# Two fused graph layers: the first layer's turns by transposing DMA instead of TensorE

## The chip, the core and the metric

The kernel runs on one core of one Trainium2 chip. The engines in the text are PE (TensorE, matrix products and transposes into PSUM), DVE (VectorE), ACT (ScalarE), POOL (GpSimd) and SP (SyncE, which here issues every DMA, in order). The metric is device time in microseconds of one execution, as the median of several runs. Trace times come from one profiled execution of the kernel.

## The reference

128 graphs of 64 nodes with 768 features pass through two layers, each of the form `layernorm(x + layer(x))`. Cut to what is computed:

```python
# layer 0: graph attention, 12 heads of 64
h = einsum('bnd,ade->bane', x, W); th = tanh(h)
attn = th @ w_src + swap(th @ w_dst)             # [b, a, n, m]
attn = where(attn >= 0, attn, 0.2 * attn)
attn = softmax(where(~adj, -999.0, attn), axis=-1)
f = elu(merge_heads(attn @ h) + b)
gate = sigmoid(x @ H_w.T + H_b)
x = layernorm(x + gate * f + (1 - gate) * x)
# layer 1: masked self-attention, 6 heads of 128
q, k, v = x @ Wq + bq, x @ Wk + bk, x @ Wv + bv
probs = softmax(q @ k.T / sqrt(128) + where(adj, 0, -9e15))
x = layernorm(x + (probs @ v) @ Wf + bf)
```

All is float32. Two graphs make a tile of 128 rows; there are 64 tiles.

## The kernel before

**Products.** The dense products are done by a Strassen-like scheme with seven products instead of eight on blocks of 128 tokens x 384 features and 384 x 384 weights. Two tiles, A and B, make a pair (32 pairs); a matrix times a pair is seven products (P1, P6, P5, P2, P7, P3, P4), each of three matmuls in the code and six PE instructions in the trace, summed in three PSUM banks. The weights' sums are prepared once: w0 and h_w by DVE, wv by POOL, and wq, wk, wf by POOL in `to_there`, which writes them to DRAM for phase B. The tokens' sums come from POOL, with DVE's help.

**Phase A** is layer 0 and the `v` of layer 1. For each pair p it emits `hidden(p)` (h and tanh, seven products, trace name h), `gate(p)` (g), and `value(p - 1)` (v). **Phase B** is the rest of layer 1, with the products q, k and o.

**The order by ticks.** The program is one hand-made order. `Beat.product` emits one product and then calls `tick`, which emits the reads of the product before and lets every open line (a generator) go on if its count is over. So a tick is the time of one product. `Beat.until(...)` ticks without emitting a product until something has been emitted. Each engine executes its own instructions in that order.

**A tile's attention** is the line `attend`, started when the last product that it needs has been read. Its steps and their ticks stand in `TICKS` (for the first pair, `FIRST_TICKS`): `targets` and `sources` on POOL; `spread`, which writes the sums to DRAM and reads them back spread over partitions (`bc`); `masked`, `greatest`, `shifts`, `lesser`, `shifted` on DVE; two exps on ACT; `greater` on DVE, whose result `d` is the softmax's numerator. Then `turn_weights` turns `d` by six PE transposes into the PSUM tile `turn` (L643), `weights` copies it to SBUF with ACT (L651), and `first_means`, `last_means` use it as the stationary operand of 24 small matmuls (`f_ps`, L665). After division, ELU, gate, sum and normalization (`normal`, ACT, L717), `turn_rows` stores the row block and turns it again by six PE transposes, and `rows` copies it into `x1b` (L727), from which `value` takes its blocks. When both tiles of a pair are turned, their sums are formed and all blocks are stored to `ops_there` for q and k.

PSUM has eight banks: four for the dense sums, two for `turn`, two for `f_ps`. The small masks and shifts of the softmax lie in unused columns of `turn`. One buffer of eight blocks (`x1b`) holds a pair's turned rows. The region `zone` in SBUF is shared by x's blocks, `to_there` and phase B's operands.

At the end of phase A the order is h31, g31, v30, then q and k of the first quad of tiles (with wq, wk and their blocks loaded from DRAM), then v31.

Of the kernel before, what the change touches and what calls it, by code (L numbers as in the profile page):

```python
# [29 lines left out]
F32 = mybir.dt.float32  # L30
U8 = mybir.dt.uint8
AF = mybir.ActivationFunctionType
ALU = mybir.AluOpType
# [39 lines left out]

TICKS = (0, 2, 2, 2, 4, 6, 7, 7, 8, 8, 10, 10, 10, 11, 12, 14, 14, 15, 15, 16, 16, 17, 18, 19, 19, 19, 20, 21, 23)

FIRST_TICKS = (0, 1, 1, 1, 3, 4, 4, 5, 5, 5, 5, 5, 5, 7, 7, 8, 8, 8, 8, 9, 9, 10, 11, 13, 13, 14, 16, 16, 16)
AFTER_A, AFTER_B = 0, 2
# [48 lines left out]
def two_layers(  # L126
# [29 lines left out]
    dram = ctx.enter_context(tc.tile_pool(name="dram", bufs=1, space=DRAM))  # L156
    dense = ctx.enter_context(tc.tile_pool(name="dense", bufs=4, space=PSUM))
    tiny = ctx.enter_context(tc.tile_pool(name="tiny", bufs=3))
# [37 lines left out]
    def to_there(w, name):  # L196
        blocks = w.rearrange("(k c p) (m n) -> k m c p n", k=2, p=P, m=2)
        for c in range(KH):
            t = in_zone(6 * D, 7, HALF)
            for at, k, m in ((W11, 0, 0), (T3, 0, 1), (W22, 1, 1), (W21, 1, 0)):  # L200
                nc.sync.dma_start(t[:, at], blocks[k, m, c])
            yield 6
            for half in (t[:, :, 0 : HALF // 2], t[:, :, HALF // 2 : HALF]):
                yield from sums_of_weights(nc.gpsimd, half)
                yield 1
            yield 3
            nc.sync.dma_start(w_there[name][:, :, c, :], t)
            yield 8

# [16 lines left out]
    def per_head(ap, k):  # L226

        return ap.unsqueeze(2).to_broadcast([P, ap.shape[1], k])

    def row(w, name, pool):  # L230
        t = pool.tile([P, w.shape[0]], F32, name=name)
        nc.sync.dma_start(t, w.partition_broadcast(P))
        return t
# [10 lines left out]
    def by_token(name, blocks, w, reads):  # L244

        sums = [sb(dense, [P, BANK], "dense", f"{name}{i}") for i in range(3)]
        begun = set()
        for what, to, xb, wb in TURNS:
            ps = sums[to][:, 0:HALF]

            def emit():
                for c in range(KH):
                    nc.tensor.matmul(  # L253
                        ps,
                        lhsT=blocks[xb][:, c, :],
                        rhs=w[:, wb, c, :],
                        start=(c == 0 and to not in begun),
                        stop=(c == KH - 1),
                        skip_group_check=True,
                    )  # L260

            read = reads[what]
            beat.product(emit, lambda read=read, ps=ps: read(ps))
            begun.add(to)
# [30 lines left out]

    ready = {}
    quads = {q: {"q": q} for q in range(n_quads)}
# [17 lines left out]
    def by_feature(name, blocks, w, f, b_sb, r, part, then=None):  # L315

        sums = [sb(dense, [P, BANK], "dense", f"{name}{i}") for i in range(3)]
        begun = set()
# [47 lines left out]
    def phase_a(pa, ps_a, dst_pool):  # L366
# [199 lines left out]
        def attend(S):  # L566
# [72 lines left out]

            def turned_from(rows):  # L640
                held["turn"] = True
                for c in range(KC):
                    nc.tensor.transpose(turn[:, c * P : (c + 1) * P], rows[:, c * P : (c + 1) * P], ident)  # L643

            def turn_weights():
                turned_from(d)


            def weights():
                S["sT"] = tmp(f"sT_{t}")  # L650
                nc.scalar.copy(S["sT"], turn[:, 0:D])  # L651
                held["turn"] = False

            def means(first, last):
                def work():
                    if first == 0:
                        held["f"] = True
                        S["f_ps"] = sb(ps_a, [P, 2 * BANK], "f", f"f_ps_{t}", 1)
                    for hd in range(first, last):
# [3 lines left out]
                        for b in range(2):  # L663
                            rows = slice(r * N, (r + 1) * N)
                            nc.tensor.matmul(  # L665
                                S["f_ps"][b * N : (b + 1) * N, at : at + E0 + 1],
                                lhsT=S["sT"][rows, hd // 2 * P + b * N : hd // 2 * P + (b + 1) * N],
                                rhs=(h[rows, hd, 0 : E0 + 1] if r == b else hx[rows, hd // 2, 0 : E0 + 1]),
# [8 lines left out]
            def divided():  # L677
                f_ps = S["f_ps"].rearrange("p (r n) -> p r n", r=2)[:, :, 0 : 6 * EP]
                f_ps = f_ps.rearrange("p r (c e) -> p r c e", c=6)
# [35 lines left out]
            def normal():  # L715
                rs = S["rs"]
                nc.scalar.activation(S["f"], S["f"], AF.Identity, bias=rs[:, 1:2], scale=rs[:, 0:1])  # L717

            def turn_rows():
                nc.sync.dma_start(x1_there[t], S["f"])  # L720
                turned_from(S["f"])

            def rows():
                if p not in x1_all:
                    x1_all[p] = sb(pa, [P, 8, KH, P], "x1b", f"x1b_{p}", 1)
                to = x1_all[p][:, 2 * side : 2 * side + 2].rearrange("p k c t -> p (k c t)")
                nc.scalar.copy(to, turn[:, 0:D])  # L727
                held["turn"] = False

            steps = [  # L730
                targets, target_sums, spread, sources, source_sums, masked, greatest, shifts, biased,
                beside, lesser, shifted, lesser_exp, shifted_exp, greater, turn_weights, weights,
                first_means, last_means, divided, below, unit, gated, summed, measured, power_of,
                normal, turn_rows, rows,
            ]

            place = {turn_weights: "turn", turn_rows: "turn", first_means: "f"}
            now = 0
            for step, at in zip(steps, TICKS if p else FIRST_TICKS):
                if at > now:  # L740
                    yield at - now
                    now = at
                while step in place and held[place[step]]:
                    yield 1
                step()
            turned[p] = turned.get(p, 0) + 1
            if turned[p] == 2:
                yield 1
                xo = x1_all[p]
                x1_blocks[p] = [xo[:, i] for i in range(8)]  # L750
                sums = xo[:, S1 : S4 + 1]
                yield from sums_of_tokens(nc.gpsimd, sums, *x1_blocks[p][0:4], first=nc.vector)
                yield 1
                there = ops_there[p // 2][:, p % 2]
                nc.sync.dma_start(there[:, 0 : 2 * KH], xo[:, 0:2].rearrange("p k c t -> p (k c) t"))
                nc.sync.dma_start(there[:, 2 * KH : 7 * KH], xo[:, 3:8].rearrange("p k c t -> p (k c) t"))

        x1_all, x1_blocks, turned = {}, {}, {}


        turn = ps_a.tile([P, 2 * BANK], F32, name="turn")
        held = {"turn": False, "f": False}

        def masks(p, A, B):
# [3 lines left out]
            for i, S in enumerate((A, B)):  # L768
                at = D + i * P
                parts = [turn[:, at : at + N]]  # L770
                parts += [turn[:, at + N + k * H0 : at + N + (k + 1) * H0] for k in range(3)]
                S["aside"], S["a8"] = parts, a8[:, i]

        def first_blocks():
            for _, _, xb, _ in TURNS:
                yield 2 if xb == S4 else 1
                blocks[xb] = load_block(0, xb)

        for p in range(n_pairs):
# [14 lines left out]
            elif p:  # L794
                beat.start(matrix("wk"), 6)
                beat.start(first_blocks())
            if p:
                beat.until(lambda: p - 1 in x1_blocks)
                value(p - 1)

        beat.until(lambda: "wq_sb" in ready and len(blocks) == 7)
        queries(0, 0, blocks, part)
        beat.until(lambda: "wk_sb" in ready)
        keys(0, 0, blocks, part)
        beat.until(lambda: n_pairs - 1 in x1_blocks)
        value(n_pairs - 1)
        beat.drain()

    blocks = {}
    with (  # L810
        tc.tile_pool(name="pa", bufs=1) as pa,
        tc.tile_pool(name="ps_a", bufs=1, space=PSUM) as ps_a,
        tc.tile_pool(name="dst_there", bufs=1, space=DRAM) as dst_pool,
        tc.manual_schedule(),
    ):
        phase_a(pa, ps_a, dst_pool)


    def phase_b(pb, ps_b):
# [3 lines left out]
        def last_bias():  # L823

            for m, parts in enumerate((((0, W11), (1, W21)), ((0, W11), (0, T1), (1, W22)))):
                ps = sb(dense, [P, BANK], "dense", f"bias_ps_{m}")[:, 0:HALF]
                steps = [(k * KH + c, wb, c) for k, wb in parts for c in range(KH)]
# [209 lines left out]
    with (  # L1037
        tc.tile_pool(name="pb", bufs=1) as pb,
        tc.tile_pool(name="ps_b", bufs=1, space=PSUM) as ps_b,
        tc.manual_schedule(),  # L1040
    ):
        phase_b(pb, ps_b)

# [46 lines left out]
```

## Time and profile before

| | |
|---|---|
| median of 2 runs | 3020.57 us (3020.05 to 3021.09) |
| profiled execution | 3020.48 us, span 3018.7 us, granted clock 0.995 |
| PE busy | 2973.2 us (98%) |
| DVE / ACT / POOL busy | 1956.1 / 778.2 / 1065.3 us |
| DMA, share of 16 engines | 36.3% on the hardware queue |
| phase A ends (last product v31) | about 1518 us |
| transposes on PE | 768 instructions, 0.27 us each, in 128 groups of six |

A group in the profile is all instructions of one line, engine and operation; `out<-in` are the program's tile names. "Idle before" is the time the engine stood before them and what released it. The chain is followed back from the last instruction to what released each step. A busy share is an average over stages: phase A and phase B have different second engines (DVE is busy 861 of 1000 us from 400 to 1400 us, and 230 of 500 from 2200 to 2700).

### The profile page before, as it was taken

What the parts mean: (1) busy time and instruction counts of PE and PEld (TensorE: products, weight loads), DVE (VectorE), ACT (ScalarE), POOL (GpSimd) and SP (SyncE); (2) the same over time, 40 slices, a digit from 0 to 9 for tenths busy, and PEclk for the clock granted to TensorE, in tenths of its full rate; (3) what the DMA queues carried; (4) which work ended last, traced back from release to release, by engine and by line L of the source; (5) the groups of instructions that cost most, each with busy time, mean ns of one, the idle gap of its engine ahead of it and who ended that gap; (6) DMA issues with size and microseconds to landing.
All of it is one profiled execution on the core that took longest, in us unless ns stands there. A gap on an engine that the chain in (4) does not pass through costs nothing.

```text
span 3018.7 us, 43164 instructions
## 1 busy us (share of the span) xinstructions
PE 2973.2 (98%) x16542; PEld 2071.7 (69%) x16542; DVE 1956.1 (65%) x3664; ACT 778.2 (26%) x1201; POOL 1065.3 (35%) x1006
## 2 busy tenths in 40 slices
PE   7999999999999999999899999999999999999998
PEld 4666666556666666666677787877878778787785
DVE  6888888888888888888634444444444454444444
ACT  2334334333333333333211111111111111111111
POOL 4556665564554554554202211112111121111212
PEclk9999999999999999999999999999999999999999
DMA  5444645534434434434741332222322223232131
GB/s 169 153 156 146 196 141 172 182 125 128 142 111 130 142 110 131 142 107 135 241 140 53 90 101 79 79 66 77 101 79 85 74 63 100 79 97 78 58 100 42
DMA packets 283311, 347.01 MB, mean 115 GB/s; under 512 B 90593, under 2 KB 226657, under 8 KB 283105
## 3 DMA queue, kind: packets, MB, share of 16 engines
q1 hardware_dynamic: 283104, 344.25, 36.3%
q8 instruction: 130, 2.13, 0.3%
q14 instruction: 77, 0.62, 0.1%
HBM read 199.07 MB, written 132.32 MB: 110 GB/s over the span
## 4 chain that ended last, share of the span: by engine, by line
PE 94%; DVE 2%; DMA 2%; issue 1%; ACT 0%; POOL 0%; SPq 0%; DVEq 0%; POOLq 0%; ACTq 0%
PE k L349 15%; PE o L253 14%; PE q L349 14%; PE h L253 14%; PE g L253 13%; PE v L253 13%; PE c_ps L907 3%; PE turn L643 3%; PE f_ps L665 2%; PE s_ps L867 2%; PE sT_ps L896 1%; DMA there<-dst 0%; DMA bc<-there 0%; DMA zone<-in_xT 0%; PE bias_ps L829 0%
## 5 line engine op out<-in xcount | busy, mean ns | idle before, releaser
L253 PE MATMUL h<-w_sb,zone 128*128 128x384 f32 x1344 | 464.2, 494 | 9.3 <-DMA w_sb<-in_w 6.7
L349 PE MATMUL q<-zone,wq_sb 128*128 128x256 f32 x2016 | 462.5, 382 | 1.6 <-DVE q_u L325 1.5
L253 PE MATMUL g<-h_w_sb,zone 128*128 128x384 f32 x1344 | 446.3, 488 | 7.5 <-DVE g L516 7.5
L349 PE MATMUL k<-zone,wk_sb 128*128 128x256 f32 x2016 | 453.6, 381 | 0.0
L253 PE MATMUL v<-wv_sb,x1b 128*128 128x384 f32 x1344 | 443.9, 489 | 8.3 <-DVE v L545 4.2
L349 PEld LDWEIGHTS q<-zone,wq_sb 128*128 128x128 f32 x2016 | 377.2, 190 | 60.2 <-DVE q_u L325 2.4
L349 PEld LDWEIGHTS k<-zone,wk_sb 128*128 128x128 f32 x2016 | 378.8, 190 | 55.5 <-DVE zone L335 4.7
L253 PEld LDWEIGHTS v<-wv_sb,x1b 128*128 128x128 f32 x1344 | 255.8, 191 | 190.9 <-issue 16.9
L253 PEld LDWEIGHTS g<-h_w_sb,zone 128*128 128x128 f32 x1344 | 251.2, 191 | 170.2 <-DVE g L516 8.1
L253 PEld LDWEIGHTS h<-w_sb,zone 128*128 128x128 f32 x1344 | 246.9, 191 | 162.2 <-issue 9.3
L947 POOL TENSOR_TENSOR y<-y,bf_sb 128x768 f32<-128x768 f32 x64 | 114.9, 1816 | 498.3 <-DMA y<-x_there 414.9
L960 POOL TENSOR_TENSOR o<-o,y 128x384 f32<-128x384 f32 x96 | 107.4, 1119 | 499.3 <-issue 250.6
L253 PE MATMUL o<-wf_sb,sc 128*128 128x384 f32 x768 | 268.0, 493 | 2.8 <-DVE sc L239 2.8
L277 POOL TENSOR_TENSOR rs<-rs,power 128x1 f32<-128x1 f32 x128 | 71.4, 558 | 538.6 <-DVE rs L275 538.6
L253 PEld LDWEIGHTS o<-wf_sb,sc 128*128 128x128 f32 x768 | 144.1, 191 | 100.0 <-DVE sc L239 3.8
L253 PE MATMUL o<-wf_sb,cT 128*128 128x384 f32 x576 | 201.8, 487 | 0.5 <-ACT cT L921 0.5
L493 POOL TENSOR_TENSOR xg<-xg,zone 128x768 f32<-128x768 f32 x64 | 134.2, 2097 | 178.1 <-ACT xg L490 178.1
L576 POOL TENSOR_TENSOR bc<-th,w_dst_sb 128x768 f32<-128x768 f32 x64 | 119.0, 1859 | 136.8 <-ACT th L466 136.8
L253 PEld LDWEIGHTS o<-wf_sb,cT 128*128 128x128 f32 x576 | 109.2, 190 | 70.7 <-ACT cT L921 1.1
L638 DVE TENSOR_TENSOR d<-d,e 128x768 f32<-128x768 f32 x64 | 84.5, 1320 | 57.0 <-ACT d L632 57.0
L593 POOL TENSOR_TENSOR th<-th,w_src_sb 128x768 f32<-128x768 f32 x64 | 116.7, 1823 | 2.4
L325 DVE TENSOR_TENSOR k_u<-k_u,k 128x256 f32<-128x256 f32 x96 | 40.2, 420 | 112.9 <-PE k L349 111.9
(148 smaller groups left out, 3969.7 us busy)
## 6 DMA issues: line engine op xcount, KB each, us to landing
zone<-ops_there SPq DMA_DIRECT2D x224, 192.0 KB, 3.9
ops_there<-x1b SPq DMA_DIRECT2D x32, 960.0 KB, 5.5
zone<-in_xT SPq DMA_DIRECT2D x32, 768.0 KB, 6.9
zone<-in_x SPq DMA_DIRECT2D x64, 384.0 KB, 4.0
bc<-there SPq DMA_DIRECT2D x128, 192.0 KB, 3.4
x_there<-f SPq DMA_DIRECT2D x64, 384.0 KB, 3.6
v_there<-v SPq DMA_DIRECT2D x128, 192.0 KB, 1.9
v<-v_there SPq DMA_DIRECT2D x128, 192.0 KB, 4.0
```

The lines of the kernel that those rows point to most:

```text
L253: nc.tensor.matmul(ps, lhsT=blocks[xb][:, c, :], rhs=w[:, wb, c, :], start=(c == 0 and to not in begun), stop=(c == KH - 1), skip_group_ch ...
L277: nc.gpsimd.tensor_tensor(rs[:, 0:1], rs[:, 0:1], power, ALU.pow)
L349: nc.tensor.matmul(ps, lhsT=w[:, wb, c, f * P : (f + 1) * P], rhs=blocks[xb][:, c, :], start=(c == 0 and to not in begun), stop=(c == KH - 1),
L493: nc.gpsimd.tensor_tensor(S["xg"], S["xg"], S["x"], ALU.mult)
L576: nc.gpsimd.tensor_tensor(bc, th, w_dst_sb, ALU.mult)
L593: nc.gpsimd.tensor_tensor(th, th, w_src_sb, ALU.mult)
L638: nc.vector.tensor_tensor(d, d, e, ALU.max)
L643: nc.tensor.transpose(turn[:, c * P : (c + 1) * P], rows[:, c * P : (c + 1) * P], ident)
L665: nc.tensor.matmul(S["f_ps"][b * N : (b + 1) * N, at : at + E0 + 1], lhsT=S["sT"][rows, hd // 2 * P + b * N : hd // 2 * P + (b + 1) * N], ...
L907: nc.tensor.matmul(c_ps[:, r, i, b * N : (b + 1) * N], lhsT=Q["v"][i][rows, b, f * E1 : (f + 1) * E1], rhs=sT[rows, i, b * N : (b + 1) * N ...
L947: nc.gpsimd.tensor_tensor(y, y, bf_sb, ALU.add)
L960: nc.gpsimd.tensor_tensor(u[k], u[of], y[:, m], ALU.add)
```

## The change

The two turns of each tile no longer use PE. A four-byte value is taken as two two-byte halves: ACT copies the tile so that all low halves and then all high halves lie together (`part_weights`, `part_rows`), one DMA on SP's queue with the transposing mode turns the 128 x 1536 two-byte array in groups of 128 columns (`turn_weights`, `turn_rows`), and ACT copies it back into interleaved halves (`weights`, `rows`). The tick lists get one more step for each turn and three to four ticks between the DMA and the copy back. They also now apply `FIRST_TICKS` to the first two pairs.

The two banks of `turn` are free: phase A has six banks for dense sums, and the masks lie in columns of one lasting tile `f_all` that also takes `f_ps`. `value` follows two pairs behind instead of one. The turned rows lie alternately in `x1_even` and in `zone` (where `to_there` makes room, working on blocks of 128 columns in 512-byte rows, nine per matrix instead of three larger ones), with one separate tile for the sums. At the end the order is h31, g31, v29, v30, q, k, v31, and the loads of wk and of the first blocks start at other ticks.

```diff
-TICKS = (0, 2, 2, 2, 4, 6, 7, 7, 8, 8, 10, 10, 10, 11, 12, 14, 14, 15, 15, 16, 16, 17, 18, 19, 19, 19, 20, 21, 23)
+TICKS = (0, 2, 2, 2, 4, 6, 7, 7, 8, 8, 10, 10, 10, 11, 12, 13, 14, 17, 18, 18, 19, 19, 20, 21, 22, 22, 22, 23, 24, 24, 28)
-FIRST_TICKS = (0, 1, 1, 1, 3, 4, 4, 5, 5, 5, 5, 5, 5, 7, 7, 8, 8, 8, 8, 9, 9, 10, 11, 13, 13, 14, 16, 16, 16)
+FIRST_TICKS = (0, 1, 1, 1, 3, 4, 4, 5, 5, 5, 5, 5, 5, 7, 7, 8, 8, 11, 11, 11, 12, 12, 13, 14, 16, 16, 17, 19, 19, 19, 22)
...
         for c in range(KH):
-            t = in_zone(6 * D, 7, HALF)
+            for q in range(KH):
+                t = in_zone(8 * D, 7, P)
...
+    def halves(ap):
+        return ap.bitcast(U16).rearrange("p (n k) -> p k n", k=2)
+    def by_halves(ap):
+        return ap.bitcast(U16).rearrange("p (k n) -> p k n", k=2)
...
-            def turned_from(rows):
-                held["turn"] = True
-                for c in range(KC):
-                    nc.tensor.transpose(turn[:, c * P : (c + 1) * P], rows[:, c * P : (c + 1) * P], ident)
+            def part_weights():
+                nc.scalar.copy(by_halves(e), halves(d))
             def turn_weights():
-                turned_from(d)
+                to = d.bitcast(U16).rearrange("p (g t) -> p g t", t=P)
+                nc.sync.dma_start_transpose(to, e.bitcast(U16))
             def weights():
-                S["sT"] = tmp(f"sT_{t}")
-                nc.scalar.copy(S["sT"], turn[:, 0:D])
-                held["turn"] = False
+                nc.scalar.copy(halves(e), by_halves(d))
...
+            def part_rows():
+                nc.sync.dma_start(x1_there[t], S["f"])
+                S["parts"], S["turned"] = tmp(f"parts_{t}"), tmp(f"turned_{t}")
+                nc.scalar.copy(by_halves(S["parts"]), halves(S["f"]))
             def turn_rows():
-                nc.sync.dma_start(x1_there[t], S["f"])
-                turned_from(S["f"])
+                to = S["turned"].bitcast(U16).rearrange("p (g t) -> p g t", t=P)
+                nc.sync.dma_start_transpose(to, S["parts"].bitcast(U16))
             def rows():
...
-                nc.scalar.copy(to, turn[:, 0:D])
-                held["turn"] = False
+                nc.scalar.copy(halves(to), by_halves(S["turned"]))
...
-            for step, at in zip(steps, TICKS if p else FIRST_TICKS):
+            for step, at in zip(steps, TICKS if p > 1 else FIRST_TICKS):
...
-                while step in place and held[place[step]]:
+                while step in place and held[place[step]] or step == rows and p > valued["pairs"] + 1:
...
-                beat.start(matrix("wk"), 6)
-                beat.start(first_blocks())
-            if p:
-                beat.until(lambda: p - 1 in x1_blocks)
-                value(p - 1)
-        beat.until(lambda: "wq_sb" in ready and len(blocks) == 7)
+                beat.start(matrix("wk"), 2)
+            if p > 1:
+                values(p - 2)
+        beat.start(first_blocks())
+        values(n_pairs - 2)
+        beat.until(lambda: len(blocks) == 7)
+        beat.until(lambda: "wq_sb" in ready)
         queries(0, 0, blocks, part)
         beat.until(lambda: "wk_sb" in ready)
         keys(0, 0, blocks, part)
-        beat.until(lambda: n_pairs - 1 in x1_blocks)
-        value(n_pairs - 1)
+        values(n_pairs - 1)
```

`values(p)` ticks until pair p's turned rows have been emitted and then emits `value(p)`.

## The prediction

> **What bounds the kernel now.** I read the page first, then the stretches of the span, the chain of work in order of time for one pair, and the waits of each engine.
>
> ```profile
> span 3018.7 us, 43164 instructions
> PE 2973.2 (98%) x16542; PEld 2071.7 (69%) x16542; DVE 1956.1 (65%) x3664; ACT 778.2 (26%) x1201; POOL 1065.3 (35%) x1006
> PE 94%; DVE 2%; DMA 2%; issue 1%; ACT 0%; POOL 0%; SPq 0%; DVEq 0%; POOLq 0%; ACTq 0%
> ```
>
> The chain that ended last is 94% TensorE (PE). What leaves PE's order leaves the time, unless something else comes last in its place.
>
> ```profile
> 400.00:1400.00 1000.00, 995.96 (x5397) 608.21 (x5396) 861.25 (x1492) 365.86 (x527) 528.06 (x474) 1.00 0.43 137
> ```
>
> Columns: PE, weight loads, DVE, ACT, POOL, then clock, DMA share, GB/s. In the long middle of phase A, PE idles 4 of 1000 us, the clock is 1.00, and DVE follows at 86%, ACT at 37%. One pair in the chain:
>
> ```profile
> 835.23 0.86 PE f_ps L665 x48
> ...
> 842.75 0.86 PE f_ps L665 x48
> 843.61 6.00 PE h L253 x18
> 849.61 0.66 PE turn L643 x6
> 850.27 5.81 PE g L253 x18
> 856.08 0.66 PE turn L643 x6
> 856.73 7.74 PE g L253 x24
> 864.47 13.54 PE v L253 x42
> 878.02 0.65 PE turn L643 x6
> 878.67 1.94 PE h L253 x6
> 880.61 0.86 PE f_ps L665 x48
> ```
>
> From 835.23 to 880.61 a pair takes 45.38 us: 21 products of 6 instructions (1.94 us each), two f_ps of 0.86, four groups of turns of 0.655. Nothing waits. Without the turns a pair is 45.38 - 4 x 0.655 = 42.76 us, and a tick (one product's time) is 42.76 / 21 = 2.04 us.
>
> **What leaves PE.** 128 groups of turns (64 tiles, weights and rows) x 0.655 = 83.8 us. The six banks add nothing to it: PE already idles 0.4% in the middle, so four banks hold up little there.
>
> **What ACT gets.** Two PSUM copies of 0.80 us per tile go (128 x 0.80), four copies of 1536 two-byte elements come. The trace has no two-byte copy.
>
> ```profile
> L651 ACT COPY sT<-turn x64: 781/799/801, 51.6 to 1481.2; 128x768 f32<-128x768 f32 x64
> ```
>
> 384 elements take 0.48 us (L541) and 768 take 0.80, so 0.32 us per 384 more: 0.80 + 2 x 0.32 = 1.44. From below 0.80, if the bytes set the time; from above 3.0, if two-byte strides halve the rate. I take 1.5, nearest to the count of elements. Per pair ACT goes from 0.366 x 45.4 = 16.6 us to 16.6 - 4 x 0.8 + 8 x 1.5 = 25.4 of 42.76 (59%); at 3.0 it is 37.4 (87%). It costs nothing by itself, since PE's first need of ACT, the copy of P1, has three products' time.
>
> **What the DMA queue gets.** Per pair four transposing transfers of 384 KB on SP's queue. None is in the trace. The bounds:
>
> ```profile
> hx<-h SPq DMA_DIRECT2D x128, 97.5 KB, 5.2
> x_there<-f SPq DMA_DIRECT2D x64, 384.0 KB, 3.6
> ```
>
> The same bytes, plain, land 3.6 us after issue (4.0 for the rows of x). hx moves 384 pieces of 260 bytes in 5.2 us; were a transpose to move 1536 such pieces at that pace, it would be 4 x 5.2 = 21 us. I take 5 us, nearer to the plain row, because 384 KB in long rows is what is read. Their cover: tile A's `greater` ended at 829.42 (DVE), the first copy would end at 831; its f_ps stood at 835.23 and moves three products later and one turn earlier, to 840.4, and the copy back takes 1.5. So the transfer has 838.9 - 831 = 7.9 us; tile B, by the same count, 7.7. The rows have four ticks, 8 us, and after them only ACT is held. At 5 us nothing waits; beyond 7.7 us PE stands at f_ps once per tile, 64 us in all for each us late.
>
> [...]
>
> **SP's order.** SP's transfers of a pair add up to about 13 us of issue. Added: four transposes (0.33 us each like the others, or up to a few us), one more ops store, and 90 more transfers of `to_there` in all (135 for 45, same bytes, 0.4 us each, spread over some 700 us). Behind `turn_rows` of A, which waits for ACT, stands `spread` of the next pair's B, and DVE's `masked` waits for it in order; it has four ticks for two transfers that land in 1.6 and 3.4 us, so 3 us of delay are free.
>
> **DVE** is unchanged at 0.861 x 45.38 = 39.1 us per pair. To it come waits that ACT forces:
>
> ```profile
> DVE d L638 <- ACT d L632: 40.7, 44, 1.7
> DVE f L698 <- ACT elu L695: 16.9, 39, 0.5
> ```
>
> Over 22 pairs that is 2.6 us per pair, 41.7 of 42.76: DVE has about 1 us left. I price the middle at 0.3 us per pair for late ACT and late `bc` (bounds 0 and 1.5), 29 x 0.3 = 9 us. The buffers with the tag tmp go from 7 to 8 per tile of rows on the same eight slots; what that makes wait is in the same 0.3.
>
> **The start.** v0 moves behind g2, and x of pair 2 is still asked for only after g1. Before, v0 hid all of this:
>
> ```profile
> 86.00 9.84 PE L253 MATMUL v<-wv_sb,x1b 128*128 128x384 f32 x30
> 96.30 4.11 PE L253 MATMUL v<-wv_sb,x1b 128*128 128x384 f32 x12 [0.46 <-DVE v L552]
> 96.33 1.21 DVE L638 TENSOR_TENSOR d<-d,e 128x768 f32<-128x768 f32 x1 [0.17 <-ACT d L632]
> 102.73 1.00 DVE L638 TENSOR_TENSOR d<-d,e 128x768 f32<-128x768 f32 x1 [1.51 <-ACT d L632]
> ```
>
> Counting ticks by hand, six pass without a product between g1 and h2, and PE's order becomes: f_ps of pair 1's A, h2's first product, f_ps of B, the rest. g1 ends at 86.0 less four turns and 1.5 us of wait, about 82. `greater` of A1 and B1 ended at 97.5 and 103.7; their chains start about 6 us earlier, so 91.5 and 97.7; copy 1.5, transfer 4 to 5, copy 1.5 make 99 and 105. PE is idle from 82 to about 106 but for 2 x 0.86 + 1.94 = 3.7 us: 20 us, of which some 3 were idle before in this stretch. Loss 17 us; bounds 8 (the chain runs ahead more) and 26 (transposes behind each other and ahead of x).
>
> **The end.** From hidden(31) to value(31) there are 28 products before the change and 35 after it, for an attend that is 5 ticks longer, so its latency fits. But 1400 to 1500 us already has 8 us of idle PE, one small transfer taking 8.57 us behind the weights' loads. Pair 31's two weight transposes are now queued among wk's loads (8.0 us to landing): two late by 3 us, 6 us; bounds 0 and 15.
>
> **The sum**, against the profiled execution's own 3020.48 (span 3018.7), 0.1 us from the median 3020.57: 3020.5 - 83.8 + 17 + 6 + 9 = 2968.7, say **2968**, 1.7% less. Own range: all at the good bounds 3020.5 - 83.8 + 8 = 2945; all at the bad ones 3020.5 - 83.8 + 26 + 15 + 43 = 3021.
>
> **Rivals.**
> 1. *The start costs little as well* (PE's order gets x of pair 2 early, or pair 1's chain runs fully ahead): 5 + 0 + 0 lost, 2942. For it: DVE idles about a quarter of the first 100 us (73.93 busy). Against: one DVE chain per tile that no tick shortens.
> 2. *DVE becomes the bound*: ACT's eight longer copies sit before the exps, its forced waits rise from 2.6 to 5, a pair is 39.1 + 5 = 44.1: 1.3 x 29 = 39 lost, 3020.5 - 83.8 + 23 + 39 = 2999. For: 1 us of slack. Against: tile B's exp no longer stands behind a copy that waits for PE (that was most of L638's 1.7 us).
> 3. *The transposes land late* (slower): one mechanism, at f_ps, 64 us for each us beyond 7.7. It makes the kernel slower than before from 7.7 + 52/64 = 8.5 us, and by 2% from 9.5 us; at 11 us, 2968 + 211 = 3180. At 21 us the queue alone needs 84 us per pair: some 4300. For it: hx's pace, a queue 43% busy. Against: the plain rows.
>
> **How the numbers follow.** Forecast 0.56, rival 1 0.15, rival 2 0.10, rival 3 0.19. About 2% (60 us) is what a measurement of this kernel can tell from no change; that line is at 2960, and a third of the forecast's chance lies below it (0.18), so faster 0.33; the rest of it and rival 2 within 2%, 0.48; slower 0.19. The range 2935 to 3100 leaves out the best of rival 1 and most of rival 3.
>
> **What would show it.** Right: no turn line on PE; f_ps waiting for nothing in the middle, a pair of 42.8 to 43.3 us; ACT copies near 1.5 us; transposes landing under 7 us; PE idle some 20 us between 80 and 110. Wrong: PE's largest wait at f_ps for ACT's copy (rival 3), products waiting for DVE all through phase A (rival 2), or no gap before h2 (rival 1).

## The result, and the profile after

The changed kernel takes 3194.1 us (3190.3 to 3197.9) against 3020.6: ratio 1.0575, 95% interval 1.052 to 1.0629. The forecast was 2968, with a range that ended at 3100: it was wrong in sign and far outside.

First the head of the page after, the shares of the chain, and the stretch from 400 to 1400 us (PE, weight loads, DVE, ACT, POOL, clock, DMA share, GB/s):

```profile
span 3196.1 us, 42114 instructions
PE 2957.6 (93%) x15774; PEld 2004.7 (63%) x15774; DVE 2029.9 (64%) x3664; ACT 1094.3 (34%) x1329; POOL 1116.5 (35%) x1042
...
PE 58%; DVE 18%; DMA 9%; ACT 7%; issue 7%; SPq 1%; POOL 0%; ACTq 0%; DVEq 0%; POOLq 0%
```

```profile
400.00:1400.00 1000.00, 885.68 (x4415) 505.88 (x4413) 821.43 (x1336) 525.75 (x557) 527.00 (x475) 0.98 0.61 159
```

The 768 PE transposes are gone (16542 less 15774), and PE is idle for 114 of 1000 us where it was idle for 4. The chain, which was 94% PE, now changes engines all the time. All of the loss is in phase A: v31 ends at about 1694 us instead of 1518, and what follows takes 1502 and 1501 us. A pair took 45.6 us before and 50.6 after (the loads of the masks, one per pair, stand at 417.55 and 1375.16 us before, 21 pairs apart, and at 412.96 and 1374.67 after, 19 apart). The prediction had 42.8 to 43.3.

The chain for one pair, in order of time (start, duration, what):

```profile
831.58 0.97 PE f_all L669 x48
...
832.89 5.86 DMA d<-e
...
840.79 0.93 PE f_all L669 x48
841.72 7.71 PE g L260 x18
...
861.25 5.19 DMA turned<-parts
...
884.35 0.93 PE f_all L669 x48
```

This pair has 52.8 us from f_all to f_all, and a piece of 18 instructions of g spans 7.71 us that spanned 5.81 before; the granted clock in this piece is 0.78 (more on that below). The waits from 400 to 1400 us (us in total, times, longest):

```profile
DVE r L685 <- PE f_all L669: 62.1, 22, 3.5
...
PE g L260 <- DVE g L523: 45.5, 19, 3.2
ACT x_even L734 <- DMA turned<-parts: 44.9, 19, 5.2
...
DVE d L645 <- ACT d L639: 36.6, 20, 3.4
ACT e L657 <- DMA d<-e: 34.4, 19, 4.0
...
PE f_all L669 <- ACT e L657: 28.8, 32, 2.7
```

DVE stands for PE once a pair (r reads f_all) and PE stands for DVE once a pair (g). Neither is full, DVE at 82%: each is late at one place and early at another, which points to the places of the work and not to its amount. The copies and transfers themselves:

```profile
L657 ACT COPY e<-d 128x1536 uint16<-128x1536 uint16 x64 | 122.2, 1909 | 56.8 <-DMA d<-e 56.8
...
L650 ACT COPY e<-d 128x1536 uint16<-128x1536 uint16 x64 | 94.2, 1472 | 82.5 <-DVE d L645 80.0
```

```profile
d<-e SPq DMA_TRANSPOSE x64, 4.8
turned<-parts SPq DMA_TRANSPOSE x64, 5.2
```

The transfers land in what was assumed (medians of 4.8 and 5.2 us for 5), the parting copy takes 1.47 us for 1.5, the copy back 1.91.

### The profile page after: what moved, and what is told of

It reads as the page before. It is cut to its first block, busy times and chain, and to the rows that moved or that the text cites. A ratio compares the mean times of both kernels' runs of the same rounds, so it can differ in the third digit from the quotient of the medians.

```text
span 3196.1 us, 42114 instructions
## 1 busy us (share of the span) xinstructions
PE 2957.6 (93%) x15774; PEld 2004.7 (63%) x15774; DVE 2029.9 (64%) x3664; ACT 1094.3 (34%) x1329; POOL 1116.5 (35%) x1042
## 4 chain that ended last, share of the span: by engine, by line
PE 58%; DVE 18%; DMA 9%; ACT 7%; issue 7%; SPq 1%; POOL 0%; ACTq 0%; DVEq 0%; POOLq 0%
PE k L356 14%; PE o L260 14%; PE q L356 14%; PE h L260 5%; DMA turned<-parts 5%; PE c_ps L933 3%; PE g L260 3%; ACT e L657 2%; PE v L260 2%; DVE f L710 2%; DVE st L277 2%; PE s_ps L893 2%; DVE d L645 2%; DMA d<-e 1%; DVE d L636 1%
## 5 line engine op out<-in xcount | busy, mean ns | idle before, releaser
L260 PE MATMUL g<-h_w_sb,zone 128*128 128x384 f32 x1344 | 488.1, 518 | 106.6 <-DVE g L523 84.6
L260 PE MATMUL h<-w_sb,zone 128*128 128x384 f32 x1344 | 454.5, 494 | 8.4 <-DMA w_sb<-in_w 6.8
L260 PEld LDWEIGHTS g<-h_w_sb,zone 128*128 128x128 f32 x1344 | 259.1, 199 | 312.4 <-DVE g L523 103.7
L260 PEld LDWEIGHTS h<-w_sb,zone 128*128 128x128 f32 x1344 | 255.8, 193 | 185.1 <-issue 12.8
L260 PE MATMUL v<-wv_sb,x_sums 128*128 128x384 f32 x768 | 265.9, 493 | 17.2 <-DVE v L559 13.3
L260 PEld LDWEIGHTS v<-wv_sb,x_sums 128*128 128x128 f32 x768 | 145.4, 192 | 126.2 <-issue 27.1
L583 POOL TENSOR_TENSOR bc<-th,w_dst_sb 128x768 f32<-128x768 f32 x64 | 128.6, 2009 | 271.0 <-ACT th L473 261.2
L657 ACT COPY e<-d 128x1536 uint16<-128x1536 uint16 x64 | 122.2, 1909 | 56.8 <-DMA d<-e 56.8
L645 DVE TENSOR_TENSOR d<-d,e 128x768 f32<-128x768 f32 x64 | 93.7, 1465 | 53.8 <-ACT d L639 53.8
L607 DVE TENSOR_TENSOR d<-bc,f_all 128x768 f32<-128x768 f32 x64 | 97.3, 1521 | 45.2 <-DMA bc<-there 24.0
```

The source lines that it names most:

```text
L260: nc.tensor.matmul(ps, lhsT=blocks[xb][:, c, :], rhs=w[:, wb, c, :], start=(c == 0 and to not in begun), stop=(c == KH - 1), skip_group_ch ...
L583: nc.gpsimd.tensor_tensor(bc, th, w_dst_sb, ALU.mult)
L607: nc.vector.tensor_tensor(dh, bc.rearrange("p (j h) -> p h j", h=H0), over_heads(mask, H0), ALU.add)
L645: nc.vector.tensor_tensor(d, d, e, ALU.max)
L657: nc.scalar.copy(halves(e), by_halves(d))
```

## The experiments

The theories, by the letters that the expectations use. H: the transfers and the long copies are late or hold ACT and SP in order. D: DVE's busy time per pair is the limit. R: the rest of the change (start, values two behind, banks). O, formed after the result and the first four experiments: the ticks put into the lists put DVE's steps at the wrong products. Q, formed after weights_on_pe: the rows' transfer is in the way of the next pair's `spread`.

**Taking out the transfers, the copies, or both.** In no_transfer the two transposing transfers go and the copies stay, so the operands stay unturned (NEG is -20 here and in no_copies, so that all numbers stay finite):

```diff
-nc.sync.dma_start_transpose(to, e.bitcast(U16))
-nc.sync.dma_start_transpose(to, S["parts"].bitcast(U16))
-nc.scalar.copy(halves(e), by_halves(d))
+nc.scalar.copy(halves(d), by_halves(e))
...
```

> Leaves out both transposing transfers (values stay unturned, and the mask's value is -20 so that no sum is zero); the four ACT copies per tile stay. Theory H (the time goes into latency: ACT stands in order behind each transfer, 5.9 us a pair, and the chain from greater over copy, transfer, copy and f_ps to divided holds DVE, which holds PE): nearly all of it comes back, 2960 to 3000 us, a pair near 43 us. Rival D (DVE's own throughput: 42.1 us of busy time a pair, slowed beside ACT's two-byte copies): the copies are all there, so 3130 or more. Rival R (the rest of the change, values two pairs behind, small blocks in to_there): unchanged, about 3190.

In no_copies the parting copies go, the weights' copy back shrinks to one element, the rows' copy is a plain one of 768, and the transfers stay (the turned values are not used):

```diff
-nc.scalar.copy(by_halves(e), halves(d))
-nc.scalar.copy(halves(e), by_halves(d))
+nc.scalar.copy(d.bitcast(U16)[:, 0:1], e.bitcast(U16)[:, 0:1])
-nc.scalar.copy(by_halves(S["parts"]), halves(S["f"]))
-nc.scalar.copy(halves(to), by_halves(S["turned"]))
+nc.scalar.copy(to, S["f"])
...
```

> Leaves out the parting copies and the copy back of the weights, and makes the copy back of the rows a plain one of 768 elements; the two transfers per tile stay, and a one-element ACT copy waits for each (values are not turned; mask value -20). Theory H: the transfers' part of the chain stays and 6 us of copies per tile go, so about half of the loss comes back, 3050 to 3110 us. Rival D: ACT's two-byte copies were what slowed DVE, so it falls to 2960 to 3000. Rival R: about 3190.

In both_on_pe both turns are PE's again, with the old places in the tick lists and four dense banks; the rest of the change stays:

```diff
-nc.sync.dma_start_transpose(to, e.bitcast(U16))
+turned_from(d)
-nc.sync.dma_start_transpose(to, S["parts"].bitcast(U16))
+turned_from(S["f"])
+TICKS, FIRST_TICKS: turn, copy and later steps where the old lists had them
```

> Both turns go back to TensorE, with the tick lists of before and four banks; values two pairs behind, FIRST_TICKS for two pairs, the small blocks of to_there and the moved loads stay. Theory H and rival D: the steady pair is 45.4 us again, only the start is worse, so 3030 to 3050 us. Rival R: well above 3100.

Measured: no_transfer 3122.9 (ratio 1.0329, 1.0299 to 1.0359), no_copies 3141.7 (1.0391, 1.0347 to 1.0436), both_on_pe 3045.6 (1.0073, 1.0044 to 1.0103). R is worth 25 us (22 against the runs of the kernel before that were made beside it, 3023.8), where the prediction had 23 for start and end. With no transfer at all the kernel is still some 100 us slower than before, and with hardly a copy some 120. H, which expected 2960 to 3000 and 3050 to 3110, does not hold by itself, and neither does D, which expected 2960 to 3000 without the copies.

**One turn at a time.** rows_on_pe gives the rows back to PE and leaves the weights to the transfer. four_banks is the change with four dense banks.

```diff
rows_on_pe, against the change:
-nc.sync.dma_start_transpose(to, S["parts"].bitcast(U16))
+turned_from(S["f"])
+TICKS = (... 13, 14, 17, 18, 18, 19, 19, 20, 21, 22, 22, 22, 23, 24, 24, 26)
four_banks, against the change:
-tc.tile_pool(name="dense_a", bufs=6, space=PSUM)
+tc.tile_pool(name="dense_a", bufs=4, space=PSUM)
```

> Only the weights go by transfer; the rows are turned by TensorE as before (four banks), the rest of the change stays. Theory H with the weights' chain as the main part (PE waits at f_all, DVE at the reciprocal, 3 us a pair each): still 3080 to 3130 us. If instead ACT's standing behind the rows' transfer (4.2 us a pair) is the main part: 3000 to 3050. Rival R: 3190.

> The change with four banks for the dense sums instead of six. Theory O: PE can run ahead of a bunched DVE by less, so slower, 3230 to 3290 us. Rival D (a steady bound): the same 3194 within 15 us. Theory H: the same.

rows_on_pe 3123.4 (1.0331, 1.0301 to 1.0361), inside H's first band. four_banks 3193.7 (1.0573, 1.0542 to 1.0604): the six banks do nothing, and O's guess on them was a miss.

**The lists alone.** gaps_on_pe is both_on_pe with the change's tick lists: PE turns, no transfer, no long copy.

```diff
against both_on_pe, from part_weights on:
-TICKS = (... 14, 14, 14, 15, 15, 16, 16, 17, 18, 19, 19, 19, 20, 21, 21, 23)
+TICKS = (... 13, 14, 17, 18, 18, 19, 19, 20, 21, 22, 22, 22, 23, 24, 24, 28)
```

> Both turns on TensorE and four banks, but with the change's tick lists and their gaps. Theory O: the bunching alone costs, though a pair of 45.4 us leaves DVE more room: 3080 to 3150 us against 3046 for the same with the old lists. Theory H and rival D: no transfers and no long copies, so 3046 to 3055.

3171.9 (1.0501, 1.0447 to 1.0554): the lists alone cost 126 us, more than O's own band (3080 to 3150), where H and D expected no loss (3046 to 3055). One pair in PE's order of time, and DVE's line where it stood longest:

```profile
805.08 0.82 PE L652 MATMUL turn<-ident,d 128*128 128x128 f32 x6
...
829.66 0.87 PE L652 MATMUL turn<-ident,f 128*128 128x128 f32 x6 [1.63 <-ACT f L726]
...
838.72 3.23 PE L260 MATMUL g<-h_w_sb,zone 128*128 128x384 f32 x6 [2.39 <-DVE g L523]
841.75 1.49 PE L652 MATMUL turn<-ident,f 128*128 128x128 f32 x6
...
856.64 0.82 PE L652 MATMUL turn<-ident,d 128*128 128x128 f32 x6
```

```profile
815.25 0.23 DVE L690 RECIPROCAL r<-f_all 128x12 f32<-128x12 f32 x1 [2.95 <-PE f_all L674]
```

From 805.08 to 856.64 are 51.56 us (the mean pair is 50.3). The excess of 5.7 over the 45.8 us of both_on_pe is four pieces: PE stands 1.63 us for `normal`'s result and 2.39 us for DVE's read of g, and just after the longer stop its work is slow (3.23 us for a product that takes 1.94, and 1.49 us for a group of turns that takes about 0.8): 1.63 + 2.39 + 1.29 + 0.67 = 6.0. The slow work is the clock: from 839.75 us on, the trace has the granted clock at half for 3.41 us (0.67 on average from 838 to 843). From 400 to 1400 us there are 11 such stretches, 37.5 us in all, which is 19 us lost of 1000; both_on_pe has none. Some 23 us before PE's stop DVE had nothing to do: 2.95 us before r. The places fit this. Counted from tile A's start, g's reads come at ticks 23 to 29. In the old list DVE's last step of tile B (`measured`, tick 19, and B is three ticks behind) came at 22, just ahead of them. Three ticks later it comes at 25, in the middle of the reads and of the next pair's sums.

weights_gap and rows_gap put in one gap at a time, both turns still on PE:

```diff
weights_gap:
+TICKS = (... 13, 14, 17, 18, 18, 19, 19, 20, 21, 22, 22, 22, 23, 24, 24, 26)
rows_gap:
+TICKS = (... 14, 14, 14, 15, 15, 16, 16, 17, 18, 19, 19, 19, 20, 21, 21, 25)
```

> Both turns on PE and four banks as in both_on_pe (3046), with the change's list only as far as the gap of the weights' turn (three ticks from the turn to its copy, all later steps three later); the rows' copy two ticks behind its turn as in the old list. If that gap is the tick lists' whole part: 3155 to 3175 as gaps_on_pe, and then rows_on_pe (3123), which differs only by the weights' transfer, gained the 42 us of 64 turns and its transfer costs nothing beyond the gap. If the gaps of weights and rows share the 126 us: 3090 to 3130.

> Both turns on PE and four banks, with weights_on_pe's list (old places up to `normal`, four ticks from the rows' turn to its copy). If the rows' part is the transfer's traffic ahead of the spread and not its gap: 3040 to 3055, as both_on_pe. If the two ticks more delay the tokens' sums and move DVE: 3080 to 3110.

weights_gap 3122.8 (1.0336, 1.0317 to 1.0355), rows_gap 3040.7 (1.0064, 1.0046 to 1.0083). The weights' gap alone costs 77 us, the rows' gap nothing, both together 49 more than the weights' alone (weights_gap falls into the lower band, rows_gap into the first). Part of the 49 is the clock: in weights_gap, PE's longest stop from 400 to 1400 us is 1.66 us and the granted clock never drops there; in gaps_on_pe stops of 2.0 to 2.7 us come once a pair. rows_on_pe differs from weights_gap by the weights' transfer only and takes the same time: the 42 us (64 x 0.655) that PE saves are eaten by transfer and copies.

**What else could lie behind the lists.** sums_on_pool moves DVE's share of the tokens' sums to POOL, gaps_no_bias takes one POOL instruction per tile away, and even_ticks is the whole change with a list that spreads DVE's work evenly by the durations of the trace:

```diff
-yield from sums_of_tokens(nc.gpsimd, so, *b, first=nc.vector)
+yield from sums_of_tokens(nc.gpsimd, so, *b)
...
-nc.gpsimd.tensor_tensor(h[:, :, 0:E0], h[:, :, 0:E0], over_heads(b0_sb, H0), ALU.add)
...
+TICKS = (0, 2, 3, 3, 5, 7, 8, 8, 8, 9, 9, 9, 9, 9, 10, 11, 11, 15, 16, 16, 17, 17, 18, 18, 19, 20, 22, 23, 25, 25, 31)
+AFTER_A, AFTER_B = 0, 3
```

> The change, with the two sums of the turned rows that DVE does moved to POOL (DVE has 2.2 to 3.4 us less a pair). Rival D: the pair shortens by that, 32 x 2.5 = 80 us, about 3110. Theory O: these sums fall ahead of the idle stretch, so little, 3150 to 3190.

> gaps_on_pe (both turns on PE, the change's tick lists, 3172) without POOL's addition of b0 to h, one POOL instruction of 1.8 us per tile; b0's share of the result is left out. If the order alone costs (DVE standing for PE and PE for DVE), POOL's work is beside the point: 3155 to 3175. If the loss is DVE's instructions growing beside POOL's (a DVE instruction on SBUF takes 1.8 us beside one of POOL and 0.6 to 1.0 us alone), two fewer of these per pair give back about 2 x 0.9 us x 29 = 50 us: 3100 to 3130.

> The whole change, with another tick list and AFTER_B 3: from the durations of the trace the list spreads DVE's work so that its backlog over a pair stays near 2 us instead of 6.7, and it gives the transfers one tick more. Theory O (the gaps for the transfers bunched DVE's steps: little to do for six ticks, then 20 us of work in seven ticks, more than PSUM's slack lets PE run ahead): most comes back, 2970 to 3030 us. Rival D (DVE's work itself grew to 42 us a pair and is the bound whatever the order): 3100 or more. Theory H (the transfers' latency on the path): 3130 or more, one tick being 2 us.

sums_on_pool 3166.6 (1.0483, 1.0453 to 1.0514): DVE falls to 777 of 1000 us and only 27 us come back, in O's band, so D as the whole cause falls. gaps_no_bias 3172.1 (1.0506, 1.0485 to 1.0527): no change, so this POOL instruction beside DVE's is not it; others were not taken away. In gaps_on_pe's trace DVE's L703 takes 0.56 us at 816.51, with POOL idle, and 1.84 us at 825.88, beside POOL's L600; L587 stays at 0.94 us at 837.26, beside another L600. even_ticks 3158.2 (1.0456, 1.0425 to 1.0486), where O had expected 2970 to 3030. DVE's wait for f_all is gone from its trace (1.5 us per 1000), but DVE now stands 47 us per 1000 before `masked` (39 of it put down to the rows' transfer), and PE 46 for v's reads. O as first put is only part of the cause.

**The rows' transfer with the old list.** In weights_on_pe the weights go back to PE, all steps up to `normal` stand at their old places, and only the rows go by transfer, with nothing of the chain behind them. weights_start adds an earlier load of pair 2's xT.

```diff
-nc.sync.dma_start_transpose(to, e.bitcast(U16))
+turned_from(d)
+TICKS = (... 14, 14, 14, 15, 15, 16, 16, 17, 18, 19, 19, 19, 20, 21, 21, 25)
weights_start besides, for p == 1 ahead of gate(p, A, B):
+early = x_blocks(2)
+next(early)
```

> Only the rows are turned by transfer (transpose and both copies, four ticks between them); the weights are turned by PE again, at the old list's places, so that from the start of the chain to `normal` every step stands where the old list had it. Theory O (the order: the ticks put in after the weights' turn shift all later DVE steps against the products' reads): the rows' transfer has nothing of DVE behind it, so its whole gain of 64 x 0.655 = 42 us shows against both_on_pe (3046): 3000 to 3020, below the kernel before, a pair of 44 us, PE waiting under 1 us per pair in the middle. Rival H (the transfers and the long copies themselves hold ACT and SP): two long copies per tile and a transfer of 5 us stay, half of what the change has: 3080 or more. Rival D (DVE's total): 39.1 us per pair are as before: 3000 to 3020 as well.

> weights_on_pe with one more edit: xT of pair 2 is asked for before g1 is emitted instead of after it, so that its sums need no spun ticks and h2 follows g1 two ticks later, not six. If the start's loss is what the spun ticks make (PE standing behind pair 1's chain), 8 to 18 us less than weights_on_pe: about 2990, and faster than the kernel before by 1%. If the start is set by pair 1's chain anyway (its f_ps are only passed from before h2 to behind it), 0 to 4 us less.

weights_on_pe 3131.2 (1.0373, 1.0357 to 1.039), weights_start 3133.4 (1.0377, 1.036 to 1.0395): 111 us over O's 3020 and in H's band (3080 or more). The trace names one wait that the kernel before hardly had, DVE's `masked` for bc, 2.4 us per tile; first the kernel before, then weights_on_pe:

```profile
DVE d L600 <- DMA bc<-there: 5.0, 4, 2.9
...
DVE d L607 <- DMA bc<-there: 97.8, 38, 4.0
```

On SP's queue around one of them (start, time on the queue):

```profile
829.15 2.39 SPq L735 DMA_TRANSPOSE turned<-parts  x1
831.63 1.30 SPq L591 DMA_DIRECT2D there<-dst  x1
835.90 1.10 SPq L594 DMA_DIRECT2D bc<-there  x2
```

`spread` writes 6 KB (there<-dst) and reads it back (bc). Its operand was ready at 829.17, but it stands behind the transposing transfer and was issued only at 831.63; the read-back, which waits for the 6 KB, could go only at 835.90. The 6 KB had landed at 835.85, just behind the transposing transfer at 835.67. So the delay has two parts. Over the tiles B from 400 to 1400 us (medians), the write is issued 3.6 us after its operand is ready and lands 2.8 us after that; from operand to landing it is 6.7 us. In both_on_pe, with the plain 384 KB of x_there ahead of it, it is issued at once and lands in 2.5, 2.6 us in all. rows_act puts the transposing transfer on ACT's queue, rows_late leaves it on SP's and moves the last three steps eight to nine ticks later:

```diff
-nc.sync.dma_start_transpose(to, S["parts"].bitcast(U16))
+nc.scalar.dma_start_transpose(to, S["parts"].bitcast(U16))
...
+LATE_TICKS = TICKS but for part_rows 29, turn_rows 30, rows 34 (21, 21, 25); for pairs 2 to 29
```

> weights_on_pe with the rows' transposing transfer on ACT's queue instead of SP's, at the same place in the order. If SP's order is what makes bc late (1.5 to 2.4 us of SP per transpose, and SP standing for ACT's copy): the wait of `masked` falls below 30 us per 1000, 3030 to 3060. If the transfer's traffic on the shared DMA engines delays the spread's packets: the wait stays above 60, 3110 to 3135 (ACT loses 1.5 to 2.4 us per tile besides).

> weights_on_pe with the last three steps of the rows moved nine ticks later for pairs 2 to 29 (part_rows 29, turn_rows 30, rows 34 in place of 21, 21, 25), so that the transposing transfer is issued after the next pair's spread has landed and been read, not just ahead of it. Theory Q (the spread's two small transfers, which DVE's `masked` waits for in order, come behind the transposing transfer on SP and share the DMA engines with it): the wait of `masked` for bc falls from 98 us per 1000 to under 15, and the kernel to 3000 to 3030, at or below the kernel before. Rival A (ACT's longer copies): they stay, and the kernel stays at 3110 to 3135.

rows_act 3131.8 (1.0365, 1.0345 to 1.0386), the same as on SP's queue:

```profile
817.05 0.33 SPq L591 DMA_DIRECT2D there<-dst  x1
823.52 1.09 SPq L594 DMA_DIRECT2D bc<-there  x2
```

SP is free and issues at once, and still 6.47 us pass until the read-back can go. The transfer issued on ACT's queue at 814.69 landed at 822.4, and x_there's 384 KB, issued at 815.78, took 7.2 us instead of 3.9 (the median of these tiles in both_on_pe). From operand to landing the 6 KB again take 6.6 us (median), now by the landing alone. So taking SP's order away gained nothing: x_there took longer beside the transposing transfer on the other queue, and the 6 KB landed behind x_there. In weights_on_pe, both_on_pe and rows_act alike they land 0.2 us (median) behind the large transfer that was issued last before them on their own queue (the transposing one in the first, x_there in the other two). What in the DMA makes it so, no run shows.

rows_late 3059.5 (1.0123, 1.0106 to 1.014): 72 us back by moving three steps, and `masked` waits 37.8 us per 1000 instead of 97.8. The write of tiles B is issued at once again and is there 2.3 us after its operand. Q is borne out for this version in its direction, not in its size: 3000 to 3030 and a wait under 15 had been expected. The two long copies on ACT moved together with the transfer, so their part in the 72 us is not separated. What was left (DVE's `greater` behind ACT's exps, 36 us, and `lesser` behind the copy back, 32) was tried in rows_tuned:

```diff
+LATE_TICKS: part_rows 33, turn_rows 34, rows 39; sums of a pair's rows 3 ticks behind, not 1; xT of pair 2 ahead of g1
```

> rows_late (3060) with the rows' last steps four to five ticks later still (33, 34, 39), the tokens' sums of a pair three ticks behind the copy instead of one, in a tick where DVE has 0.5 us of other work, and xT of pair 2 asked for before g1. The wait of `masked` for bc should fall from 38 to some 10 us per 1000, that of `greater` for the exp from 36 to under 15: 25 to 40 us back, 3020 to 3035; all of it would be 3004. If ACT's long copies hold the order wherever they are put: 3050 to 3065.

3072.8 (1.0173, 1.0159 to 1.0187), a miss: the wait for bc stayed (39 us per 1000), and `greater` waited 41 times instead of 24, 35 us in all as before. No version of this change that ran is faster than the kernel before.

**The same move in the whole change.** change_late is the change, even_late is even_ticks, with the last three steps later:

```diff
change_late:
+LATE_TICKS = TICKS but for part_rows 32, turn_rows 33, rows 37 (24, 24, 28); for pairs 2 to 29
even_late:
+LATE_TICKS = TICKS but for part_rows 31, turn_rows 32, rows 36 (25, 25, 31); for pairs 2 to 29
```

> The whole change, with the rows' last three steps nine ticks later for pairs 2 to 29 (32, 33, 37 for 24, 24, 28). If the transfers' part is the collision of the rows' transfer with the spread, it goes here too and the tick list's part stays: gaps_on_pe less the turns, 3172 - 84 = 3088, to 3120. If DVE's order with the shifted list hides that part (in the whole change `masked` waits only 9 us per 1000 for bc), nothing moves: 3180 to 3200.

> even_ticks (the whole change with a tick list that spreads DVE's work evenly, 3158, DVE waiting 47 us per 1000 before `masked`) with the rows' last three steps six to seven ticks later for pairs 2 to 29. Theory Q: the wait before `masked` goes, 47 x 1.4 = 66 us back, 3080 to 3110; what is left over is PE's wait for v's and g's reads. Rival A: 3150 to 3165.

change_late 3182.2 (1.0532, 1.0511 to 1.0553), even_late 3174.6 (1.0507, 1.0486 to 1.0528). In the whole change the move gives 12 us (in the second band), and on the even list it costs 16 (above both bands). There, in even_late, the wait before `masked` goes, and 80 us of DVE's reads of h behind ACT's copy and 51 us of PE's f_all behind the copy back come in its place. In the change itself there was little to gain: `spread` of tiles B is issued at once (median 0.03 us after its operand, landed after 2.3), and `masked` waits 8.6 us per 1000 for bc.

## Why the prediction was wrong

**The sum, as measured.** In us, from runs that each add one part of the change:

| term | forecast | measured |
|---|---|---|
| profiled time before | 3020.5 | 3020.5 |
| turns leave PE | -83.8 | -83.8 taken over (768 instructions are gone; no run measures it alone) |
| start and end, values two behind | +23 | +25 (both_on_pe less before; some 7 of it in the middle: 45.83 less 45.60 us in 29 pairs) |
| the tick lists | not costed | +126 (gaps_on_pe less both_on_pe) |
| transfers and copies in that order | +9 | +106 (the rest, to 3194.1) |

The last line is a remainder: gaps_on_pe and the change differ by 22 us, and with the 83.8 that the turns should have saved that is 106. Taking out only the transfers gives back 71, only the long copies 52; together that is more than the remainder, and no run leaves out both while the turns stay off PE.

**The step that failed** is the sentence "DVE is unchanged", with "about 1 us left" and a price of 0.3 us a pair, bounds 0 and 1.5, 9 us in the sum. It compared busy time per pair (39.1 of 42.76) and did not ask where in the pair the time lies. Measured, a pair lost 50.6 - 42.8 = 7.8 us, five times the upper bound, although DVE was busy only 82%. The tick lists stood in the diff; every step behind `weights` moved three ticks against the reads of g, and none of it was in the sum: with both turns on PE these lists alone cost 126 us. Of the 7.8 us PE stands still for 5.8 (114 of 1000 us); the other 2 are slower work, and half of that is the granted clock, which is at half for 41 of these 1000 us and was never lowered there before.

DVE was not unchanged in size either: 39.3 us a pair before (0.861 x 45.6), 41.2 in both_on_pe (0.898 x 45.83), 41.6 after (0.821 x 50.6). Against 42.76 this alone leaves little, even with every step in its best place.

**ACT** was right in size: copies of 1.47 and 1.91 us for 1.5, 26.6 us a pair (0.526 x 50.6) for 25.4. That it costs nothing by itself was not: without the long copies 52 us come back. DVE's forced wait for the exps did not grow: 40.7 us per 1000 before, 36.6 after.

**The transfers** were right in size, 4.8 and 5.2 us for 5. They hold SP for 2.2 and 2.5 us (medians; 1.3 to 4.6), so of the prediction's two values, 0.33 us like the other transfers or "up to a few us", the second came out, for which the profile before has no row. That nothing waits at 5 us failed: f_all waits for the copy back in 32 places, 28.8 us per 1000.

**SP's order** looked at the right place (`spread` behind `turn_rows`, 3 us of slack), but counted only issue time. In weights_on_pe the small write is there 6.7 us after its operand instead of 2.6, 4.1 us late: it is issued 3.6 us after its operand (median), and it lands 0.2 us (median) behind the transposing transfer ahead of it. Moving the transfer out of its way gave back 72 us there. In the whole change `spread` is not late.

**The start and the end** came out at 25 us for 17 + 6, but in part by luck. In both_on_pe the loads of the masks of pairs 4 and 31 stand at 199.3 and 1437.6 us (before: 189.1 and 1420.6), with one v (13.5 us) less done at both. So the start costs 10.2 + 13.5 = 24 us, near its upper bound of 26, the middle 7, and the end gains 5 where 6 were priced (v31 ends at 1543.6 for 1517.9). The picture of the start after the change:

```profile
89.09 4.21 PE L260 MATMUL g<-h_w_sb,zone 128*128 128x384 f32 x6 [7.67 <-DVE g L523]
...
104.17 0.34 PE L669 MATMUL f_all<-h,e 64*64 64x65 f32 x1 [10.87 <-ACT e L657]
```

PE stands 7.67 us for DVE before g1's last product and 10.87 us at pair 1's first f_all; it is idle for 19.5 of the 30 us from 80 to 110, as the prediction had it (some 20). Asking for xT earlier (weights_start against weights_on_pe) moved nothing, which fits a start set by the chain and not by the load.

**Banks**: that six add nothing was right (four_banks).

**The rivals.** Rival 2 had the signature, products waiting for DVE all through phase A, but by ACT's forced waits, which did not rise, and at 1.3 us a pair. Rival 3 had the sign and the size (3180 at 11 us), but its mechanism is only a small part: the transfers mostly stayed under its 7.7 us, and PE's wait at f_all for the copy back, 28.8 us per 1000, is less than that for g (45.5). Rival 1 is out: the start cost more than was said.

**What stays open.** Why no list that was tried is good for the whole change: each removed the wait that it was made for and got another (even_ticks v and `masked`, even_late h and f_all). The interplay of the order on DVE, ACT and PE was not taken apart further, and the remainder of 106 us is split between transfers and copies only roughly. No run has the whole change with the old lists. Why DVE's instructions took longer already in both_on_pe was not followed up.

## What to carry to other kernels

Where a program's order is written by hand, a step that is moved by a few ticks moves everything behind it on every engine: lay the busy time of the second engine out tick by tick before and after, since a mean of 82% hides stretches that are full and stretches that are empty. A latency of 5 us that replaces 0.66 us of work is paid in the order, even where the data is in time: the three ticks made for it cost 77 us with no transfer at all (weights_gap). And keep small transfers that an engine waits for away from a large one: from operand to landing the 6 KB of `spread` took 6.7 us behind the transposing transfer on the same queue (weights_on_pe) and 6.6 with it on the other queue (rows_act), against 2.6 without it (both_on_pe).

## What the runs showed of the hardware

- A 6 KB write landed 0.2 us (median) after the 384 KB transfer issued before it on the same queue, transposing (weights_on_pe) or plain (both_on_pe, rows_act). Issued after an x_there that ran beside a transposing transfer on the other queue, it took 6.5 us (rows_act); after an x_there alone 2.5 (both_on_pe, tiles B), with no large transfer ahead of it 1.4 (both_on_pe, tiles A).
- In the changed kernel the transposing transfers of 384 KB land in 4.8 and 5.2 us (medians; 3.7 to 8.4), a plain one of the same size in 4.1; they hold the issuing queue 2.2 and 2.5 us (medians; 1.3 to 4.6), where x_there holds it 0.3 to 0.6.
- In the changed kernel a two-byte copy of 128 x 1536 on ACT takes 1.47 us where every second element is read (L650, L726) and 1.91 to 1.93 us where every second one is written (L657, L734).
- In gaps_on_pe PE's first product after a stop of 2.4 us took 3.23 us instead of 1.94, and the group of turns after it 1.49 instead of about 0.8, with the granted clock at half for 3.41 us from 839.75 on. In gaps_on_pe and in the change the granted clock dropped to half 11 times each from 400 to 1400 us, always at a stop of PE of 1.97 us or more or within 1.5 us after it, though not at every such stop; it never dropped there in before, both_on_pe, rows_gap, weights_gap and rows_late, whose stops are at most 1.78 us.
